# Raw patch sets in two transfers of 64 and 8 rows, borders on GpSimd, a first root of one column

## The chip, the cores and the metric

The kernel runs on one core of a Trainium2 chip. The metric is the device time of one execution in microseconds (us); the time of a kernel is the median of its runs.

## The reference

The input is a batch of 16 images of 256 channels, 28x28 pixels, in float32. Two layers replace a 3x3 convolution by soft look-up in a table: each channel's 3x3 patch is compared with 16 centroids of that channel, a softmax over the negative distances gives 16 weights, and these weigh 16 rows of a table, summed over all channels.

```python
def amm_conv3x3(x, centroids, w_sub):
    p = patches(x, 3x3, 'SAME')                        # (B, HW, C, 9)
    d = sum(p*p, -1) - 2*einsum('bncs,cks->bnck', p, centroids) + sum(centroids**2, -1)
    attn = softmax(-d, axis=-1)                        # over the 16 centroids
    lut = einsum('cks,cso->cko', centroids, w_sub)
    return einsum('bnck,cko->bno', attn, lut)          # back to (B, C, 28, 28)

h   = groupnorm(x, 32 groups, eps=1e-5)
out = relu(bn1(amm1(h)))
out = bn2(amm2(out))
out = out * sigmoid(relu(mean_hw(out) @ w1 + b1) @ w2 + b2)
result = x + relu(out + h)
```

## The kernel before

The work is cut into blocks: one image, one half of the channels (`hh`, 128 partitions) and one half of the rows (`t`, 14 rows of 28 pixels, 392 columns). `BLOCKS = ((0, 0), (0, 1), (1, 1), (1, 0))` is the order of the (hh, t) blocks of an image. In this text block 0 to block 3 are those of image 0 in layer 1, with which the program begins.

A block goes through these steps:

- Two *patch sets* (`p` 0 and 1) of 128 partitions x 3136 elements: nine taps of eight channel groups. Later blocks build them by DMA from a padded image (`patches`, L549). 
- `logits` (L578): matmuls of the patches with the centroid weights into PSUM (`lg`); `exps` (L589) on ScalarE gives `e`.
- `num_b` (L643) and `num_a` (L629): the matmuls `nb` and `na` on `e`, which form sums over centroids and numerators. `split_r`, `split_q` on ScalarE and `join_r`, `join_q` (L657, L668) on VectorE take `nb` apart; `recip` (L671), `spread` (L682, L686, shuffles) copy the reciprocal to the partitions; `scale_a` (L705, VectorE) and `scale_q` (L694, GpSimd) make the normalised weights `qp`, `qo`. `scale_a` reads `na` from PSUM and so frees its bank.
- `mix` (L720, L722, GpSimd) adds pairs of these, since the last product with the table, `product` (L713, into `acc`), is done by a scheme of seven products instead of eight on a 2x2 split; `combine` (L237, VectorE) adds table pieces for the same scheme.

**Image 0 of layer 1 is different.** Its patches are not of the normalised image: they are the raw input, laid out beforehand in `in_p0` and loaded as eight sets by `raw` (L268 to L273), and the group norm is folded into the logit weights: `tap_scale` (L397) multiplies the weights by each channel's root, `tap_shift` (L405, L408) takes the mean out of them. Nine taps of eight channels take 72 of the 128 partitions; `RAW` lists as (first row, step) which rows one transfer fills, and the constant `TAPS` which of the 16 rows of a group hold taps. A patch at the image's edge must see zero after the norm, so its raw value must be the mean: `border` (L485 to L494) adds it, once to the first and last column (L489) and once to the first or last row (L491), both on VectorE. The statistics are made by `raw_stats`, `raw_mean`, `raw_dev`, `raw_var`, `raw_means`, `raw_norm` and `raw_keep` (L427 to L483), for `k` 0 and 1, the two halves of the channels; the root is a power of -0.5 (`mhalf`) on GpSimd, of 16 columns in `raw_norm` (L473) and of one in `raw_keep` (L481). Sets 0 and 1 (block 0) and 4 to 7 (blocks 2 and 3) go into the two patch buffers, sets 2 and 3 (block 1) into the space of the table buffers `wall`.

**What sets the order.** Each engine runs its instructions in the order of the program. The start is written out by hand; then every step is entered in a list under a key (block and a fraction of it), and the program walks the sorted list. `QUEUE` holds the keys at which SyncE (SP) issues sets 2 to 7, and `BORDER` those of the eight borders. An SP issue waits while eight earlier transfers are outstanding, and for its buffer to be free. PSUM banks go by a table of tags (`EARLY`), so a block's logits wait until the last reader of their bank is done. Around these steps stand the group norm of image 1 (`gn_stats`, `gn_mean`, `gn_var` with a root at L311 and L312, `to_home1` L547) and `setup_bn` (L311, L312 on GpSimd, then L320 to L328 on VectorE: the constants of the two batch norms), entered at (6, 2.75); `keep_wd` (L411) issues two DMAs from GpSimd.

Of the kernel before, what the change touches and what calls it, by code (L numbers as in the profile page):

```python
# [12 lines left out]
ALU = mybir.AluOpType  # L13
# [4 lines left out]
P = 128  # L18
# [70 lines left out]
def kernel(  # L89
# [55 lines left out]
    def bank(name, step=None, role=None, tag=None):  # L145
        return banks(name, step, role, tag)[:, 0, :]
# [4 lines left out]
    def view(t, off, dims):  # L151
        return bass.AP(t.tensor, t.offset + off, [list(d) for d in dims])
# [274 lines left out]
    def raw_stats(k):  # L427
        gn_stats(0, k)
        rr = piece(48).rearrange("p (a n) -> p a n", a=3)
        mv = gst[0][1][:, k, :]  # L430
        for i in range(2):
# [8 lines left out]
    def raw_dev(k):  # L440
        ps, rr, mean = raws["ps", k], raws["rr", k], gst[0][1][:, k, 0:1]
        dv = piece(2)
        nc.vector.tensor_sub(dv[:, 0:1], ps[:, 0:1], mean)
        nc.vector.scalar_tensor_tensor(dv[:, 1:2], ps[:, 0:1], mean, dv[:, 0:1], op0=ALU.subtract, op1=ALU.mult)
        nc.vector.scalar_tensor_tensor(rr[:, 0], hot_sb[:, :16], dv[:, 1:2], rr[:, 2], op0=ALU.mult, op1=ALU.add)
        raws["dv", k] = dv

    def raw_var(k, ps):
        nc.tensor.matmul(ps[:, :16], lhsT=eighth, rhs=raws["rr", k][:, 0], start=True, stop=True)
        nc.tensor.matmul(ps[:, 16:17], lhsT=gmat, rhs=raws["dv", k][:, 1:2], start=True, stop=True)  # L450
        raws["pv", k] = ps

    def raw_means(k):
        ps = raws.pop(("ps", k))
        m2 = piece(16)
        nc.vector.tensor_scalar(m2, ps[:, 16:32], 2.0, None, op0=ALU.mult)
        term = piece(64).rearrange("p (a n) -> p a n", a=4)
        nc.vector.tensor_tensor(
            term, ps[:, 16:32].unsqueeze(1).to_broadcast([P, 4, 16]), hot_sb[:, 16:20].unsqueeze(2).to_broadcast([P, 4, 16]),
            ALU.mult,  # L460
        )
        gm = piece(2)
        nc.vector.tensor_copy(gm, ps[:, :2])
        raws["m2", k], raws["term", k], raws["gm", k] = m2, term, gm

    def raw_norm(k):
        ve = piece(18)
        ps = raws.pop(("pv", k))
        nc.vector.tensor_scalar(ve[:, :17], ps[:, :17], GN_EPS, None, op0=ALU.add)
# [3 lines left out]
        nc.gpsimd.tensor_tensor(sc, ve[:, :16], mhalf, ALU.pow)  # L473
        nc.gpsimd.tensor_scalar(scm, sc, hot_sb[:, 22:23], hot_sb[:, 23:24], op0=ALU.mult, op1=ALU.add)
        nc.gpsimd.tensor_tensor(ms, raws["m2", k], sc, ALU.mult)
        raws["scm", k], raws["ms", k], raws["ve", k] = scm, ms, ve

    def raw_keep(k):
        ve, gm = raws["ve", k], raws["gm", k]
        rstd, shift = (nrm[:, 0, i, k : k + 1] for i in (1, 2))  # L480
        nc.gpsimd.tensor_tensor(rstd, ve[:, 17:18], mhalf[:, :1], ALU.pow)  # L481
        nc.gpsimd.tensor_tensor(shift, gm[:, 0:1], rstd, ALU.mult)
        nc.gpsimd.tensor_scalar(shift, shift, -1.0, None, op0=ALU.mult)  # L483

    def border(u, p):  # L485
        v = flat(u["pt", p]).rearrange("p (s r w) -> p s r w", s=8, w=W)
        tm, t = raws["term", u["hh"]], u["t"]
        cols = v[:, :, :, 0 : W : W - 1]
        nc.vector.tensor_tensor(cols, cols, view(tm, 8 * p, [tm.ap[0], [1, 8], [0, RT], [16, 2]]), ALU.add)  # L489
        row = v[:, :, (RT - 1) * t, :]  # L490
        nc.vector.scalar_tensor_tensor(  # L491
            row, row, hot_sb[:, 20 + t : 21 + t], tm[:, 2 + t, 8 * p : 8 * p + 8].unsqueeze(2).to_broadcast([P, 8, W]),
            op0=ALU.mult, op1=ALU.add,
        )  # L494
# [694 lines left out]
    def at(cl, sub, f, *a, **kw):  # L1189
        jobs.setdefault((cl, sub), []).append((f, a, kw))  # L1190
# [260 lines left out]
    raw_mean(0, bank("gnp", tag=0))  # L1451
    raw_dev(0)
    sq_sum(0, 0, bank("sqp", tag=1)[:, :256])
    raw_var(0, bank("gnq", tag=3))
    sq_sum(0, 1, bank("sqp", tag=2)[:, :256])
    raw_means(0)
    sq_add(0, 0)
    raw_norm(0)
    nc.gpsimd.memset(alts[0], 1.0)
    for t in xpads:  # L1460
        nc.gpsimd.memset(t, 0.0)
    raw_keep(0)
    mean_off(0, 0, 256)
    tap_sum(0, 0, bank("tap", tag=0)[:, :256])
    sq_add(0, 1)
# [5 lines left out]
    at(-0.4, 0.6, tap_shift, 0, 1)  # L1471

    def later():
        b = banks("sqp", tag=1)
# [113 lines left out]
def _lay_out(inputs):  # L1588
# [97 lines left out]
```

## Time and profile before

| | |
|---|---|
| median of 3 runs | 2619.93 us (2618.88 to 2620.37) |
| profiled execution | 2617.88 us |
| its span | 2616.4 us |
| mean granted clock of TensorE | 0.998 |
| instructions | 85872 |

In the profile PE is TensorE's matmul, DVE is VectorE, ACT ScalarE, POOL GpSimd, and SPq SyncE's DMA queue. A row of a timeline gives the start and the busy time in us, the engine, the line, the operation, output and inputs with their shapes and the number of instructions (x), and in brackets how long the engine had been idle and what it waited for. A row of the table by stretch gives the stretch, its length, the busy time and the number of instructions of each engine, the clock that was granted to TensorE as a share of full speed, the share of the DMA engines' time in use, and GB/s. Names of `first` are pieces of one constant tile; weights, terms and scales all lie there.

### The profile page before, as it was taken

Reading aid. Unit: us, or ns where it says so; the run is one execution under the profiler, and the core shown is the slowest. Engines: PE = TensorE matmul, PEld = TensorE weight load, DVE = VectorE, ACT = ScalarE, POOL = GpSimd, SP = SyncE. Lnnn points to the kernel's source line nnn. Section 1 sums busy time; section 2 is a strip of 40 time slices with the busy share of each in tenths; the row PEclk is TensorE's granted clock in tenths of the full one; section 3 lists DMA queues with packets and bytes.
Section 4 is the critical chain, followed back from the end, with each engine's and each line's share of the span. In section 5 each row is a group of like instructions: output and inputs, shape, how many; then the busy total and the mean of one; then the engine's idle time right before and its main releaser. Section 6 shows DMA issues by size and latency. Waiting matters only on the chain.

```text
span 2616.4 us, 85872 instructions
## 1 busy us (share of the span) xinstructions
PE 2591.2 (99%) x37026; PEld 1272.7 (49%) x37026; DVE 1786.9 (68%) x3812; ACT 1368.6 (52%) x1912; POOL 1900.2 (73%) x1323
## 2 busy tenths in 40 slices
PE   7999999999999999999999999999999999999999
PEld 3444454444444444444444444444444444444445
DVE  8776656666566665666666776767777667767676
ACT  5444444444444444444454655565555555555565
POOL 5786666766568766676667777778878788787776
PEclk9999999999999999999999999999999999999999
DMA  7566656665556565655664444444444444444442
GB/s 206 136 166 177 198 149 185 170 176 173 145 144 153 168 186 174 175 145 152 170 170 107 112 115 117 130 115 113 107 130 120 121 118 106 116 128 126 116 105 66
DMA packets 213672, 372.07 MB, mean 142 GB/s; under 512 B 29880, under 2 KB 183912, under 8 KB 212712
## 3 DMA queue, kind: packets, MB, share of 16 engines
q1 hardware_dynamic: 206968, 333.75, 48.0%
q0 software_dynamic: 6176, 32.66, 3.4%
q8 instruction: 295, 4.83, 0.8%
q14 instruction: 89, 0.73, 0.1%
q10 hardware_dynamic: 144, 0.10, 0.0%
HBM read 288.46 MB, written 77.95 MB: 140 GB/s over the span
## 4 chain that ended last, share of the span: by engine, by line
PE 98%; DVE 1%; issue 0%; ACT 0%; DMA 0%; POOL 0%; ACTq 0%; DVEq 0%; POOLq 0%
PE acc L713 52%; PE lg L578 17%; PE na L629 14%; PE nb L643 14%; ACT e L589 0%; PE sep L1014 0%; DMA pt<-in_p 0%; POOL qp L722 0%; PE sep L1006 0%; DVE rb L686 0%; DMA xt<-in_x 0%; PE tap L390 0%; PE sqp L374 0%; PE sqp L343 0%; DVE qp L705 0%
## 5 line engine op out<-in xcount | busy, mean ns | idle before, releaser
L713 PE MATMUL acc<-qp,wall 128*128 128x392 f32 (+1 forms) x3088 | 1100.1, 499 | 0.6 <-issue 0.3
L589 ACT ACTIVATE e<-lg 128x784 f32<-128x784 f32 x960 | 737.5, 821 | 644.2 <-PE lg L578 641.5
L722 POOL TENSOR_TENSOR qp<-qp,qp 128x784 f32<-128x784 f32 x512 | 943.7, 1866 | 159.6 <-DVE qp L705 159.2
L713 PEld LDWEIGHTS acc<-qp,wall 128*128 128x128 f32 x3088 | 569.6, 190 | 507.4 <-issue 59.5
L686 DVE STREAM_SHUFFLE rb<-r 128x392 f32<-128x392 f32 x1024 | 550.8, 604 | 0.0
L578 PE MATMUL lg<-pt,wd 32*32 32x392 f32 x15872 | 468.9, 499 | 1.0 <-issue 1.0
L657 DVE SCALAR_TENSOR_TENSOR r<-nb,kst,r 128x392 f32<-128x392 f32 x128 | 80.1, 626 | 446.2 <-ACT r L653 445.6
L705 DVE TENSOR_TENSOR qp<-na,rb 128x784 f32<-128x784 f32 x352 | 333.8, 972 | 61.2 <-PE na L629 50.0
L629 PE MATMUL na<-e,cwa 64*32 64x392 f32 x8192 | 374.1, 492 | 0.0
L643 PE MATMUL nb<-e,cwb 64*32 64x392 f32 x8192 | 373.5, 492 | 0.4 <-ACT e L589 0.3
L694 POOL TENSOR_TENSOR qo<-qo,rb 128x392 f32<-128x392 f32 x128 | 132.5, 1035 | 296.1 <-DVE rb L682 295.7
L671 DVE RECIPROCAL r<-r 128x392 f32<-128x392 f32 x128 | 333.2, 2603 | 4.4
L694 POOL TENSOR_TENSOR qp<-qp,rb 128x784 f32<-128x784 f32 x160 | 295.9, 1860 | 3.2 <-issue 0.4
L643 PEld LDWEIGHTS nb<-e,cwb 64*32 64x32 f32 x8192 | 189.4, 107 | 175.1 <-issue 21.1
L629 PEld LDWEIGHTS na<-e,cwa 64*32 64x32 f32 x8192 | 182.6, 106 | 182.5 <-issue 74.4
L578 PEld LDWEIGHTS lg<-pt,wd 32*32 32x32 f32 x15872 | 116.1, 103 | 266.1 <-issue 230.2
L713 PE MATMUL acc<-qp,w_A 128*128 128x392 f32 x512 | 183.9, 502 | 0.0
L653 ACT ACTIVATE r<-nb,kst 128x392 f32<-128x392 f32 x128 | 86.7, 677 | 166.2 <-PE nb L643 158.6
L613 POOL TENSOR_TENSOR z<-z,mx 128x1568 f32<-128x1568 f32 x32 | 91.8, 2870 | 94.8 <-DVE mx L607 94.8
L713 PE MATMUL acc<-qo,wall 128*128 128x392 f32 (+1 forms) x386 | 158.0, 491 | 0.0
L699 ACT COPY qp<-na 128x784 f32<-128x784 f32 x160 | 130.0, 813 | 21.7 <-PE na L629 20.2
L713 PEld LDWEIGHTS acc<-qp,w_A 128*128 128x128 f32 x512 | 95.3, 191 | 83.0 <-DVE qp L705 19.8
(229 smaller groups left out, 1706.8 us busy)
## 6 DMA issues: line engine op xcount, KB each, us to landing
pt<-home SPq DMA_DIRECT2D x744, 209.0 KB
pt<-home SPq DMA_DIRECT2D x744, 104.5 KB
home<-xpad SPq DMA_DIRECT2D x30, 899.0 KB
xt<-in_x SPq DMA_DIRECT2D x30, 784.0 KB
out_dram<-y SPq DMA_DIRECT2D x31, 392.0 KB
pt<-in_p SPq DMA_DIRECT2D x24, 196.0 KB
d_wS<-st SPq DMA_DIRECT2D x12, 192.0 KB
wall<-d_wS SPq DMA_DIRECT2D x4, 576.0 KB
```

What stands on the lines that cost most here:

```text
L578: nc.tensor.matmul(bk[32 * c : 32 * c + 32, :N].rearrange("p (r w) -> p r w", w=W), lhsT=(wx[u["hh"]] if early(u) else wts["wd", u["hh"]]) ...
L589: nc.scalar.activation(eg[:, 2 * i : 2 * i + 2, :], bk[:, :, :N], AF.Exp, scale=2.0)
L613: nc.gpsimd.tensor_tensor(zk, zk, mx.unsqueeze(2).to_broadcast([P, N // 4, K]), ALU.subtract)
L629: nc.tensor.matmul(bs[32 * i : 32 * i + 32, r, :N], lhsT=wts["cwa", u["hh"]][64 * r : 64 * r + 64, mm, i, :], rhs=es[64 * r : 64 * r + 64, ...
L643: nc.tensor.matmul(bs[32 * i : 32 * i + 32, r, :N], lhsT=wts["cwb", u["hh"]][64 * r : 64 * r + 64, mm, i, :], rhs=es[64 * r : 64 * r + 64, ...
L671: nc.vector.reciprocal(u["r"], u["r"])
L686: nc.vector.stream_shuffle(rb[:, r, :], u["r"], mask_of(2 * mm + r))
L694: nc.gpsimd.tensor_tensor(q, q, u.pop(("rb", mm)), ALU.mult)
L699: nc.scalar.copy(pair(u, mm), u.pop(("na", mm))[:, :, :N])
L705: nc.vector.tensor_mul(pair(u, mm), u.pop(("na", mm))[:, :, :N], rb)
L713: nc.tensor.matmul(accs[key][:, : cols[1] - cols[0]], lhsT=wl[w][:, k, :], rhs=us["q", k][:, cols[0] : cols[1]], start=first and n == 0, s ...
L722: nc.gpsimd.tensor_tensor(pair(out_u, mm), pair(in0, mm), pair(in1, mm), ALU.subtract)
```

## The change

1. A raw set comes in two transfers of 64 and 8 rows instead of four of 16 and one of 8. The 72 rows and the bytes are the same; the taps sit in other rows of their group of 16.
2. Of the eight borders, seven go to GpSimd, as three additions each: the columns without the corner row (128 x 8 x 13 x 2), the row without its ends (128 x 8 x 26) and the two corners (128 x 8 x 2), for which the table of terms has eight planes instead of four. The border of block 0's first set stays on VectorE as it was. The keys of five borders and of the issue of set 6 change.
3. The root of the first half of the channels (`k` 0) is taken of one column per partition (`raw_root`), then spread to 16 columns by a matmul and scaled by VectorE (`raw_scales`). The second half keeps the root of 16 columns. Three memsets of GpSimd move.

```diff
-RAW = ((0, 8), (4, 8), (1, 8), (5, 8), (2, 16))
+RAW = ((0, 2), (1, 16))
...
-QUEUE = (None, None, (-0.9, 0.0), (-0.4, 0.0), (0, 1.5), (1, 1.5), (4, 1.5), (5, 1.5))
-BORDER = ((-0.5, 0.0), (-0.3, 0.0), (1, 0.97), (1, 1.9), (2, 1.6), (4, 0.5), (5, 1.1), (7, 0.2))
+QUEUE = (None, None, (-0.9, 0.0), (-0.4, 0.0), (0, 1.5), (1, 1.5), (4, 0.35), (5, 1.5))
+BORDER = ((-0.5, 0.0), (-0.3, 0.0), (1, 0.5), (1, 0.98), (2, 0.5), (3, 1.5), (4, 0.82), (6, 2.72))
...
-TAPS = ((0, 8, 5), (4, 12, 13), (1, 9, 2))
+TAPS = ((0, 8, 6), (4, 12, 14), (2, 10, 1))
...
-    eighth = piece(P)
+    eighth = hpads[1][:, :P]
...
+    def raw_root(ps):
+        ve, gm = piece(2), raws["gm", 0]
+        rr, rstd = raws["rr", 0], nrm[:, 0, 1, 0:1]
+        nc.tensor.matmul(ps[:, :1], lhsT=gmat, rhs=raws["dv", 0][:, 1:2], start=True, stop=True)
+        sq_add(0, 0)
+        nc.vector.scalar_tensor_tensor(ve[:, 0:1], ps[:, :1], GN_EPS, gm[:, 1:2], op0=ALU.add, op1=ALU.add)
+        nc.gpsimd.tensor_tensor(rstd, ve[:, 0:1], mhalf[:, :1], ALU.pow)
+
+    def raw_scales(ps):
+        rr, rstd = raws["rr", 0], nrm[:, 0, 1, 0:1]
+        nc.vector.tensor_scalar(rr[:, 0], hot_sb[:, :16], rstd, None, op0=ALU.mult)
+        nc.tensor.matmul(ps[:, 16:32], lhsT=eighth, rhs=rr[:, 0], start=True, stop=True)
+        sq_add(0, 1)
+        scm, ms = piece(16), piece(16)
+        nc.vector.tensor_scalar(scm, ps[:, 16:32], hot_sb[:, 26:27], hot_sb[:, 27:28], op0=ALU.mult, op1=ALU.add)
+        nc.vector.tensor_tensor(ms, ps[:, 16:32], raws["m2", 0], ALU.mult)
+        raws["scm", 0], raws["ms", 0] = scm, ms
...
     def border(u, p):
         v = flat(u["pt", p]).rearrange("p (s r w) -> p s r w", s=8, w=W)
         tm, t = raws["term", u["hh"]], u["t"]
-        cols = v[:, :, :, 0 : W : W - 1]
-        nc.vector.tensor_tensor(cols, cols, view(tm, 8 * p, [tm.ap[0], [1, 8], [0, RT], [16, 2]]), ALU.add)
+        first = u["hh"] == 0 and t == 0 and p == 0
+        r0, r1 = (0, RT) if first else (1 - t, RT - t)
+        eng = nc.vector if first else nc.gpsimd
+        cols = v[:, :, r0:r1, 0 : W : W - 1]
+        eng.tensor_tensor(cols, cols, view(tm, 8 * p, [tm.ap[0], [1, 8], [0, r1 - r0], [16, 2]]), ALU.add)
         row = v[:, :, (RT - 1) * t, :]
...
+        eng.tensor_tensor(
+            row[:, :, 1 : W - 1], row[:, :, 1 : W - 1],
+            tm[:, 2 + t, 8 * p : 8 * p + 8].unsqueeze(2).to_broadcast([P, 8, W - 2]), ALU.add,
+        )
+        ends = row[:, :, 0 : W : W - 1]
+        eng.tensor_tensor(ends, ends, view(tm, 16 * (4 + 2 * t) + 8 * p, [tm.ap[0], [1, 8], [16, 2]]), ALU.add)
```

On GpSimd, from the second root (of 16 columns) to the root of image 1's group norm, there stood before:

```order
27 L473 TENSOR_TENSOR first<-first,mhalf 128x16
28 L474 TENSOR_SCALAR first<-first,hot_sb 128x16
29 L475 TENSOR_TENSOR first<-first 128x16
30 L397 TENSOR_TENSOR first<-wd_174,first 128x512
31 L481 TENSOR_TENSOR nrm<-first,mhalf 128x1
32 L482 TENSOR_TENSOR nrm<-first,nrm 128x1
33 L483 TENSOR_SCALAR nrm<-nrm 128x1
34 L1507 MEMSET hpad 128x900 x2
35 L694 TENSOR_TENSOR qo_198<-qo_198,rb_559 128x392
36 L694 TENSOR_TENSOR qp_186<-qp_186,rb 128x784
37 L694 TENSOR_TENSOR qp_189<-qp_189,rb 128x784
38 L311 TENSOR_SCALAR rs_t<-gn_var 128x2
```

and on the same engine there stand now, from the last addition of the border of block 2's first set to the same root:

```order
42 L525 TENSOR_TENSOR pt_68<-pt_68,first 128x8x2
43 L725 TENSOR_TENSOR qo_192<-qo_192,rb_542 128x392
44 L725 TENSOR_TENSOR qp_180<-qp_180,rb 128x784
45 L725 TENSOR_TENSOR qp_183<-qp_183,rb 128x784
46 L512 TENSOR_TENSOR pt_69<-pt_69,first 128x8x13x2
47 L520 TENSOR_TENSOR pt_69<-pt_69,first 128x8x26
48 L525 TENSOR_TENSOR pt_69<-pt_69,first 128x8x2
49 L1537 MEMSET hpad 128x900 x2
50 L512 TENSOR_TENSOR pt_68<-pt_68,first 128x8x13x2
51 L520 TENSOR_TENSOR pt_68<-pt_68,first 128x8x26
52 L525 TENSOR_TENSOR pt_68<-pt_68,first 128x8x2
53 L311 TENSOR_SCALAR rs_t<-gn_var 128x2
```

The borders of block 2 (row 42 ends the first, rows 46 to 48 are the second) now stand around block 1's scalings (L725), and the border of block 3's first set (rows 50 to 52) ahead of the root of image 1; the memset of `hpad` moved behind the scalings. Before, nothing stood between the scalings and that root. The border of block 3's second set stands behind the mixes and the two DMA issues, ahead of the batch norm's constants:

```order
62 L753 TENSOR_TENSOR qp_180<-qp_184,qp_180 128x784
63 L411 DMA d_wd_113<-wd_159 128x512
64 L411 DMA d_wd_113<-wd_168 128x512
65 L512 TENSOR_TENSOR pt_69<-pt_69,first 128x8x13x2
66 L520 TENSOR_TENSOR pt_69<-pt_69,first 128x8x26
67 L525 TENSOR_TENSOR pt_69<-pt_69,first 128x8x2
68 L311 TENSOR_SCALAR rs_t<-vecs 128x2
69 L312 TENSOR_TENSOR bnsc_953<-rs_t,mhalf 128x2
```

so that VectorE's L326, which waits for those constants, comes behind that border too, and block 2's scalings (L736, the L705 of before) behind L326:

```order
79 L326 TENSOR_TENSOR bnsc_953<-bnsc_953,vecs 128x2
80 L327 TENSOR_TENSOR bnsh_954<-vecs,bnsc_953 128x2
81 L328 TENSOR_TENSOR bnsh_954<-vecs,bnsh_954 128x2
82 L326 TENSOR_TENSOR bnsc_961<-bnsc_961,vecs 128x2
83 L327 TENSOR_TENSOR bnsh_962<-vecs,bnsc_961 128x2
84 L328 TENSOR_TENSOR bnsh_962<-vecs,bnsh_962 128x2
85 L736 TENSOR_TENSOR qp_189<-na,rb 128x784
```

These VectorE rows follow each other as they did before; what moved is the GpSimd work that the first of them waits for.

More of the change, by code (lines that the diff above doesn't have):

```diff
@@ L430, in raw_stats @@
         mv = gst[0][1][:, k, :]
-        for i in range(2):
+        for i in range(1 + k):
             nc.vector.tensor_scalar(rr[:, 1 + i], hot_sb[:, :16], mv[:, i : i + 1], None, op0=ALU.mult)
@@ L444, in raw_dev @@
         nc.vector.scalar_tensor_tensor(dv[:, 1:2], ps[:, 0:1], mean, dv[:, 0:1], op0=ALU.subtract, op1=ALU.mult)
-        nc.vector.scalar_tensor_tensor(rr[:, 0], hot_sb[:, :16], dv[:, 1:2], rr[:, 2], op0=ALU.mult, op1=ALU.add)
-        raws["dv", k] = dv
+        if k:
+            nc.vector.scalar_tensor_tensor(rr[:, 0], hot_sb[:, :16], dv[:, 1:2], rr[:, 2], op0=ALU.mult, op1=ALU.add)
+        gm = piece(2)
+        nc.vector.tensor_copy(gm, ps[:, :2])
+        raws["dv", k], raws["gm", k] = dv, gm
     def raw_var(k, ps):
@@ L1453 @@
     sq_sum(0, 0, bank("sqp", tag=1)[:, :256])
-    raw_var(0, bank("gnq", tag=3))
+    ps = bank("gnq", tag=3)
+    raw_root(ps)
+    nc.gpsimd.memset(alts[0], 1.0)
     sq_sum(0, 1, bank("sqp", tag=2)[:, :256])
     raw_means(0)
[L1457 to L1462, printed above, removed]
     mean_off(0, 0, 256)
+    raw_scales(ps)
     tap_sum(0, 0, bank("tap", tag=0)[:, :256])
-    sq_add(0, 1)
     mean_off(0, 256, 512)
@@ L1471 @@
     at(-0.4, 0.6, tap_shift, 0, 1)
+    for t in xpads:
+        at(-0.2, 0.0, nc.gpsimd.memset, t, 0.0)
+    at(-0.2, 0.1, raw_keep, 0)
     def later():
@@ L1502 @@
     for t in hpads:
-        at(1, 1.95, nc.gpsimd.memset, t, 0.0)
+        at(3, 1.55, nc.gpsimd.memset, t, 0.0)
     for key in sorted(jobs):
@@ L1630, in _lay_out @@
         hot[p, 16:20] = dx == 0, dx == 2, dy == 0, dy == 2
-        hot[p, 20:22] = dy != 0, dy != 2
-        hot[p, 22:24] = p % 16 in rows, p % 16 not in rows
+        hot[p, 20:24] = dx == 0 or dy == 0, dx == 2 or dy == 0, dx == 0 or dy == 2, dx == 2 or dy == 2
+        hot[p, 24:26] = dy != 0, dy != 2
+        hot[p, 26:28] = p % 16 in rows, p % 16 not in rows
     for n, p in enumerate(p for first, step in RAW for p in range(first, P, step)):
```

25 lines of the change are left out of this document (13 added, 12 removed).

## The prediction

> **What bounds the kernel now.** I read the busy shares first.
>
> ```profile
> PE 2591.2 (99%) x37026; PEld 1272.7 (49%) x37026; DVE 1786.9 (68%) x3812; ACT 1368.6 (52%) x1912; POOL 1900.2 (73%) x1323
> ```
>
> TensorE works 2591.2 of 2616.4 us, so an edit pays only where PE stands idle or runs slow. The second view is the busy time of each engine by stretch, cut at the first 120 us, where all edits lie.
>
> ```profile
> core 0: us, PE busy (x) PEld busy (x) DVE busy (x) ACT busy (x) POOL busy (x), PEclk, DMA share, GB/s
> 0.00:14.40 14.40, 6.30 (x16) 3.71 (x16) 9.30 (x26) 7.90 (x5) 9.50 (x20) 1.00 0.81 203
> 14.40:22.10 7.70, 7.12 (x136) 3.41 (x136) 4.24 (x12) 5.93 (x8) 3.31 (x6) 1.00 1.06 277
> 22.10:33.30 11.20, 9.37 (x197) 3.76 (x196) 10.75 (x29) 5.84 (x8) 6.57 (x9) 1.00 0.97 231
> 33.30:42.20 8.90, 6.51 (x132) 2.52 (x133) 8.73 (x18) 3.41 (x5) 5.30 (x4) 1.00 0.98 260
> 42.20:53.40 11.20, 10.85 (x87) 5.37 (x87) 9.98 (x28) 3.89 (x6) 0.97 (x2) 0.85 0.47 146
> 53.40:64.40 11.00, 7.53 (x193) 3.01 (x192) 10.96 (x17) 6.13 (x8) 8.42 (x7) 1.00 0.55 167
> 64.40:77.50 13.10, 13.04 (x142) 5.73 (x142) 10.01 (x27) 4.83 (x7) 6.43 (x9) 0.74 0.61 161
> 82.40:120.00 37.60, 37.60 (x541) 18.59 (x542) 27.86 (x65) 16.85 (x24) 33.55 (x21) 1.00 0.59 154
> ```
>
> From 82.4 us PE is never idle (37.60 of 37.60); what the change moves there passes to the end unaltered. Before that VectorE is the full engine (10.75 of 11.20, 8.73 of 8.90, 10.96 of 11.00), and GpSimd has room in the same stretches: 6.57, 5.30, 0.97, 8.42. DMA is full until about 42 us (shares 0.97 and 0.98) and half full after. Two stretches have a lower clock. Third, PE's own timeline: the logit groups behind each gap (idle before them in brackets), and two stages behind the last.
>
> ```profile
> 14.44 5.67 PE L578 MATMUL lg<-pt,first 32*32 32x392 f32 x128 [2.37 <-issue]
> 26.38 2.76 PE L578 MATMUL lg<-wall,first 32*32 32x392 f32 x64 [0.82 <-issue]
> 33.35 0.95 PE L578 MATMUL lg<-wall,first 32*32 32x392 f32 x32 [1.00 <-ACT qp L699]
> 42.21 1.81 PE L578 MATMUL lg<-pt,first 32*32 32x392 f32 x48 [2.35 <-issue]
> 64.47 3.42 PE L578 MATMUL lg<-pt,first 32*32 32x392 f32 x64 [3.54 <-issue]
> 74.72 2.86 PE L629 MATMUL na<-e,cwa 64*32 64x392 f32 x64
> 77.52 1.00 PE L578 MATMUL lg<-pt,first 32*32 32x392 f32 x32
> ```
>
> The gaps total 10.08 us (2.37 + 0.82 + 1.00 + 2.35 + 3.54), which is what there is to win, plus the clock:
>
> ```profile
> 45.00:46.00 1.00, 1.00 (x9) 0.48 (x2) 1.00 (x1) 0.80 (x2) 0.00 (x0) 0.50 0.00 0
> 70.00:71.00 1.00, 1.00 (x3) 0.62 (x2) 1.00 (x5) 0.00 (x0) 0.35 (x1) 0.50 0.87 273
> ```
>
> Behind the gap of 2.35 PE ran part of the stretch 42.2 to 53.4 at half clock (mean 0.85: 0.15 x 11.2 = 1.7 us lost), behind that of 3.54 part of the next (mean 0.74: 0.26 x 13.1 = 3.4 us lost).
>
> **The start.** The root of 16 columns becomes one of one column.
>
> ```profile
> 8.72 2.94 POOL L473 TENSOR_TENSOR first<-first,mhalf 128x16 f32<-128x16 f32 x1 [3.75 <-DVE first L469]
> 12.16 0.42 DVE L397 TENSOR_TENSOR first<-wd,first 128x256 f32<-128x256 f32 x1 [1.37 <-POOL first L474]
> 16.69 0.60 POOL L481 TENSOR_TENSOR nrm<-first,mhalf 128x1 f32<-128x1 f32 x1
> ```
>
> One column costs 0.60 against 2.94, a gain of 2.34. Against it stands a new detour, a small DVE product, one matmul and two DVE reads of PSUM before the weights can be scaled, which I put at 1.5 us together with the DVE work queued between. So the first logits start about 0.8 earlier, at 13.7 (bounds: 0, if DVE's queue eats it, and 1.4, since VectorE's scaling waited 1.37 for GpSimd here).
>
> **The borders.** Seven of eight move from DVE (two instructions) to GpSimd (three).
>
> ```profile
> 37.44 1.54 DVE L489 TENSOR_TENSOR pt<-pt,first 128x224 f32<-128x224 f32 x1
> 39.01 1.80 DVE L491 SCALAR_TENSOR_TENSOR pt<-pt,hot_sb,first 128x224 f32<-128x224 f32 x1
> 41.24 0.42 DVE L408 TENSOR_TENSOR first<-first,tmp 128x256 f32<-128x256 f32 x1
> 49.00 0.56 DVE L489 TENSOR_TENSOR pt<-pt,first 128x224 f32<-128x224 f32 x1
> 49.59 0.45 DVE L491 SCALAR_TENSOR_TENSOR pt<-pt,hot_sb,first 128x224 f32<-128x224 f32 x1
> 61.19 2.18 DVE L489 TENSOR_TENSOR pt<-pt,first 128x224 f32<-128x224 f32 x1
> 29.81 0.22 POOL L475 TENSOR_TENSOR first<-first 128x16 f32<-128x16 f32 x1
> 35.62 1.02 POOL L694 TENSOR_TENSOR qo<-qo,rb 128x392 f32<-128x392 f32 x1 [1.90 <-DVE rb L682]
> ```
>
> On DVE a border costs 1.01 alone (0.56 + 0.45), and 3.34 at 37.44 (1.54 + 1.80). On GpSimd no border stands in the trace. A line through the rows of 16 and 392 elements gives 0.22 + 192 x 0.0021 = 0.63 for 208 elements, so 0.63 + 0.63 + 0.22, about 1.5 for cols, row and corner ends. Bounds: 1.0, DVE's time alone, and 3.3, DVE's longest; I take 1.5, since the GpSimd rows are the nearest in kind. The Trainium skill, "GPSIMD Engine Reference", section 4.1, keeps elementwise work on VectorE and calls GpSimd about twice as slow with two inputs; by that a border would cost 2.0 instead of 1.5, and the sum below would lose 1 us, two borders standing in its last chain. The row of 392 elements says less, 1.02 on GpSimd.
>
> **The sets.** Five transfers of a set become two of the same 903 KB.
>
> ```profile
> 24.45 0.49 SPq L272 DMA_DIRECT2D pt<-in_p  x1
> 28.84 0.33 SPq L212 DMA_DIRECT2D cwa<-in_cwa  x1
> 45.65 3.05 SPq L272 DMA_DIRECT2D pt<-in_p  x5
> ```
>
> SP held its issues at 24.45 and 28.84 until the sets of block 1 had landed: 4.39 us a set. No 64-row transfer of these rows is in the trace. With the engines full, the bytes set the pace, so I take the same 4.4 a set (bounds 3.3, 903 KB at the 277 GB/s of the busiest stretch, and 5.9, at the 154 GB/s of the last one). The issue time falls from 3.05 to about 1.2 a set, and two transfers rather than five count towards the outstanding ones, so SP issues earlier. That hurries nothing while DMA is full. For block 3's first set another thing counts: it goes into the buffer that block 2's first logits read, was issued at 45.65 when they ended, and they will end at about 41.8 (below). It then lands between 46.2 (41.8 + 4.4) and 50.1 (45.65 + 4.4); I take 49.6, since weights stand ahead of it in the queue.
>
> **Walking PE through it.** Block 1, first set: lands 24.4, GpSimd border to 26.0, logits 26.1 (was 26.38); the start's 0.8 shrinks to 0.3, because the set is now the limit. Second set: border done 30.4, so the gap of 1.00 closes (-1.3). Block 2, first set: before, DVE did its border (37.44 to 40.8) ahead of the last tap shifts (L408, 41.24), and both stood before logits at 42.21. Now DVE is rid of it, and GpSimd goes landed set, second root (2.9), tap scale (1.05), shift, border: 30.4 to 37.8. Logits at 38.6, -3.6, and the drop to half clock behind that gap goes too (1.7). Two stalls take its place: 1.2 us at the PSUM bank that DVE's join empties, and 1.0 at the group norm of image 1, whose DVE steps stand where they stood. So block 2's second set is at -4.2. Block 3, first set: before, the border ran on DVE at 61.19 behind products, shuffles and the combine (end 64.4); now it is done by 51.1, and PE goes straight on: 57.0 instead of 64.47, -7.5. The na group behind it comes at 64.0 instead of 74.72: -10.7, with 3.4 of clock.
>
> There the gain meets a new chain. Its order on GpSimd: border of block 3's first set, image 1's root and shift, three mixes, a scaling, two mixes, two DMA issues, border of the second set, the BN constants; then DVE's L326, behind which the scalings L736 are queued, which free the banks for block 3's second logits.
>
> ```profile
> 52.33 0.25 POOL L311 TENSOR_SCALAR rs_t<-gn_var 128x2 f32<-128x2 f32 x1 [11.77 <-DVE gn_var L526]
> 53.74 0.24 POOL L529 TENSOR_SCALAR nrm<-nrm 128x2 f32<-128x2 f32 x1
> 56.33 6.63 POOL L722 TENSOR_TENSOR qp<-qp,qp 128x784 f32<-128x784 f32 x3 [2.35 <-DVE qp L705]
> 67.01 1.24 POOL L411 DMA_DIRECT2D d_wd<-wd  x2
> 69.64 0.71 POOL L312 TENSOR_TENSOR bnsc<-rs_t,mhalf 128x2 f32<-128x2 f32 x1
> 71.16 0.16 DVE L326 TENSOR_TENSOR bnsc<-bnsc,vecs 128x2 f32<-128x2 f32 x1
> 75.72 0.97 DVE L705 TENSOR_TENSOR qp<-na,rb 128x784 f32<-128x784 f32 x1 [2.45 <-PE na L629]
> ```
>
> Border done 51.1; root and shift 1.65 (52.33 to 53.98): 52.8. Mixes to DMA issues, 11.92 (56.33 to 68.25) less 0.6, since the border that ran beside them on DVE is gone: 64.1. Border 1.5: 65.6. BN constants 2.1 (68.25 to 70.35): 67.7. The second L326 with its two followers, 0.6, and one L736, 0.97: 69.3. PE has finished na at 66.85 (64.0 + 2.86), so it waits 2.4, and block 3's second logits start at 69.3 against 77.52: **-8.2**. A gap of 2.35 was followed by half clock and gaps up to 1.00 were not, so this one likely costs 1.7 again: **-6.5**.
>
> Against the profiled execution (2617.88, span 2616.4) that is 2611.4. The median of the runs, 2619.93, lies 2.05 above it; the same gain from there gives **2613.4**.
>
> **The rivals.** *A, the sets land faster* (bound 3.3 us a set): block 1 no longer waits for its sets (1.1 us more, the start's 0.8 kept and more), the second root and block 2 follow, and PE keeps some of the -10.7 at na. GpSimd's mixes still need products that DVE makes, so it ends 2 us better, and the shorter gap may spare the 1.7 of clock: 2.0 + 1.4 beyond the forecast, about 2610. For it: fewer waits on SP. Against: the engines were full, and the bytes are the same.
>
> *B, the borders on GpSimd are dearer, or the clock falls for longer.* Each us more per border costs 2 in the last chain (two borders), and the gap of 2.4 grows with it. With 2.3 a border, 1.6 us less, and 3.4 instead of 1.7 of clock: gain 3.2, or 2616.7. For it: four-dimensional views of two elements inside have no row here. What else bears on it are the stretched DVE borders beside GpSimd's scaling, 3.34 for 1.01. The Trainium skill, "SBUF — State Buffer", section "Who interferes with whom", says that a DVE instruction with two SBUF inputs and a GpSimd one that reads SBUF share a port pair, held for a whole instruction by whichever was first; by it the GpSimd borders would be stretched in their turn by DVE's adds. The trace agrees as far as DVE goes (L489 2.18 beside mixes, 0.56 alone).
>
> *C, slower: GpSimd stands at the border of block 3's first set.* All mixes are queued behind this border, which before they were not. If 64-row transfers run at 5.9 us a set instead of 4.4, seven sets (itself the last) bring it from 49.6 to 60.1; its border ends at 61.6, and root, mixes, issues, border, constants and L736 (18.2, from 51.1 to 69.3 above) give logits at 79.8, +2.3. PE waits several us just ahead of that, and a drop like that of 3.4 follows: +5.7, about 2625.6. It decides from about 5.5 a set: seven times the 1.1 then eats the 6.5 to 8.2. Against: the transfers of before used a full queue, and one of 64 rows has enough rows for 16 engines.
>
> *D, no change at all*, the first wait being another: speaks against it that DVE, the engine unloaded, is full in each of the stretches with gaps. It would leave 2619.9.
>
> **How the numbers follow.** Forecast 0.48 at 2613.4; A 0.15 at 2610; B 0.20 at 2616.7 and D 0.05 at 2619.9; C 0.12 at 2625.6. About 0.2% (5.2 us) is what a measurement of this kernel can tell from no change: faster is below 2614.7, slower above 2625.2. Of the forecast's own spread, an unsure 1 us on each of start, borders and mixes, a sixth falls above 2614.7: faster 0.40 + 0.15 = 0.55. Same: 0.08 + 0.25 and the milder part of C (0.02) = 0.35; slower 0.10. The range 2608.5 to 2621 leaves out C and the far end of A.
>
> **What would show it.** Right: the logit groups at 14.44, 26.38, 42.21 and 64.47 move to about 13.7, 26.1, 38.6 and 57.0, with no half clock near 45; a PE gap of 2 to 3 us ahead of block 3's second logits, released by DVE's scaling, and GpSimd without a pause from its border to the BN constants. A GpSimd border sums to about 1.5. Wrong: SP's issues show over 5 us a set, or GpSimd idles behind a DMA ahead of block 3's border (C); a border of 2.5 us or more (B); no gap ahead of block 3's second logits (A).

## The result

The changed kernel takes 2613.17 us (median of 9 runs, 2611.14 to 2614.54) against 2620.28 us of the kernel before beside it (9 runs): a ratio of 0.9974, 95% interval 0.9965 to 0.9984. Run again beside other kernels it took 2612.87 us against 2617.00, a ratio of 0.998 (0.9971 to 0.9989). The profiled execution took 2614.36 us, its span 2612.9. The number came out as forecast, but by another sum: the start had the wrong sign, the sets were faster than the sum has them, a loss of clock was charged that this profile does not show, and these errors nearly cancelled.

PE's timeline of the changed kernel, the logit groups of the first blocks and the na group behind block 3's first (L609 and L660 are the L578 and L629 of before):

```profile
16.58 6.27 PE L609 MATMUL lg<-pt,first 32*32 32x392 f32 x128 [1.67 <-issue]
27.71 2.78 PE L609 MATMUL lg<-wall,first 32*32 32x392 f32 x64
40.99 1.82 PE L609 MATMUL lg<-pt,first 32*32 32x392 f32 x48
43.77 0.89 PE L609 MATMUL lg<-pt,first 32*32 32x392 f32 x16 [0.96 <-DVE qo L699]
59.20 2.77 PE L609 MATMUL lg<-pt,first 32*32 32x392 f32 x64
66.71 2.86 PE L660 MATMUL na<-e,cwa 64*32 64x392 f32 x64
71.75 0.95 PE L609 MATMUL lg<-pt,first 32*32 32x392 f32 x32 [2.19 <-issue]
```

Against the rows of before the first logits are 2.1 late, those of block 1 1.3 late, block 2's 1.2 early, block 3's first 5.3 early, the na group 8.0 early, and block 3's second logits 5.8 early (71.75 for 77.52). The gaps of 2.35 and 3.54 ahead of blocks 2 and 3 are gone; one of 2.19 stands ahead of the last row, where none was. The table by stretch shows the clock:

```profile
core 0: us, PE busy (x) PEld busy (x) DVE busy (x) ACT busy (x) POOL busy (x), PEclk, DMA share, GB/s
13.40:21.20 7.80, 5.91 (x103) 2.86 (x105) 6.35 (x16) 2.97 (x4) 4.08 (x7) 1.00 0.97 338
21.20:24.60 3.40, 3.37 (x59) 1.74 (x50) 0.11 (x1) 3.15 (x5) 1.70 (x3) 1.00 0.96 296
45.00:53.00 8.00, 7.69 (x65) 3.92 (x71) 7.42 (x26) 1.27 (x3) 2.63 (x6) 1.00 0.34 115
66.70:76.60 9.90, 7.32 (x165) 2.90 (x164) 7.50 (x19) 3.68 (x6) 8.10 (x10) 1.00 0.41 138
76.60:120.00 43.40, 43.37 (x596) 21.73 (x604) 31.30 (x78) 18.55 (x26) 37.33 (x25) 1.00 0.61 156
```

Both stretches of low clock are gone, and in this profile the gap of 2.19 was not followed by a new one (1.00 in the fourth row). From 76.6 us to 120 PE is busy throughout (43.37 of 43.40), so the 5.8 us pass on there. The other new thing is in the last column: with DMA just as full, the sets move at 338 and 296 GB/s, where it was 277 and 231.

At the start the row that matters is VectorE's L477, the spread of the root to 16 columns in `raw_scales` (one tile times one column as the scalar operand):

```profile
8.30 0.58 POOL L473 TENSOR_TENSOR nrm<-first,mhalf 128x1 f32<-128x1 f32 x1 [3.34 <-DVE first L472]
8.85 2.89 POOL L1487 MEMSET wall<- 128x3360 f32 x1
9.13 2.64 DVE L477 TENSOR_SCALAR first<-hot_sb,nrm 128x16 f32<-128x16 f32 x1
9.27 2.50 DVE L379 TENSOR_TENSOR wd<-wd,sqp 128x256 f32<-128x256 f32 x1
```

The root takes 0.58, as costed. But L477, 16 columns, takes 2.64 us and ends at 11.77, just behind GpSimd's fill of a table buffer (L1487, 8.85 to 11.74), with L379, the next instruction, behind it. The borders and the chain ahead of block 3's second logits:

```profile
21.21 0.96 POOL L512 TENSOR_TENSOR wall<-wall,first 128x208 f32<-128x208 f32 x1 [2.58 <-DMA wall<-in_p]
22.25 0.54 POOL L520 TENSOR_TENSOR wall<-wall,first 128x208 f32<-128x208 f32 x1
22.74 0.25 POOL L525 TENSOR_TENSOR wall<-wall,first 128x16 f32<-128x16 f32 x1
24.60 0.95 POOL L512 TENSOR_TENSOR wall<-wall,first 128x208 f32<-128x208 f32 x1 [1.61 <-DMA wall<-in_p]
50.38 0.94 POOL L512 TENSOR_TENSOR pt<-pt,first 128x208 f32<-128x208 f32 x1 [5.21 <-PE gnp L547]
54.67 6.65 POOL L753 TENSOR_TENSOR qp<-qp,qp 128x784 f32<-128x784 f32 x3 [0.91 <-DVE qp L736]
69.47 0.71 POOL L312 TENSOR_TENSOR bnsc<-rs_t,mhalf 128x2 f32<-128x2 f32 x1
70.22 0.16 DVE L326 TENSOR_TENSOR bnsc<-bnsc,vecs 128x2 f32<-128x2 f32 x1 [0.45 <-POOL bnsc L312]
70.69 2.73 DVE L736 TENSOR_TENSOR qp<-na,rb 128x784 f32<-128x784 f32 x3
```

A border costs 1.8 us (21.21 to 22.99), and the sets of block 1 land 3.4 us apart (24.60 less 21.21: GpSimd waits for each), not 4.4. The chain is the one that was forecast: constants, L326, the scaling L736, then PE. One wait in it was not: GpSimd stands 0.91 us for VectorE's products (L736) ahead of the mixes at 54.67.

### The profile page after: what moved, and what is told of

Same layout as the page of the kernel before. It is cut to its first block, busy times and chain, and to the rows that moved or that the text cites. A ratio compares the mean times of both kernels' runs of the same rounds, so it can differ in the third digit from the quotient of the medians.

```text
span 2612.9 us, 85829 instructions
## 1 busy us (share of the span) xinstructions
PE 2590.2 (99%) x37026; PEld 1273.7 (49%) x37026; DVE 1779.5 (68%) x3798; ACT 1369.3 (52%) x1912; POOL 1908.8 (73%) x1341
## 3 DMA queue, kind: packets, MB, share of 16 engines
q8 instruction: 295, 4.83, 0.8%
## 4 chain that ended last, share of the span: by engine, by line
PE 97%; DVE 1%; POOL 1%; issue 0%; ACT 0%; DMA 0%; SPq 0%; ACTq 0%; POOLq 0%
PE acc L744 52%; PE lg L609 17%; PE nb L674 14%; PE na L660 14%; POOL qp L753 0%; DVE rb L717 0%; DVE r L702 0%; PE sep L1045 0%; ACT e L620 0%; PE sep L1037 0%; DMA xt<-in_x 0%; DVE gn_st L424 0%; DVE qp L736 0%; DVE first L477 0%; PE tap L390 0%
## 5 line engine op out<-in xcount | busy, mean ns | idle before, releaser
L609 PE MATMUL lg<-pt,wd 32*32 32x392 f32 x15872 | 470.1, 499 | 1.0 <-DMA pt<-home 0.4
L660 PE MATMUL na<-e,cwa 64*32 64x392 f32 x8192 | 374.3, 492 | 0.0
L736 DVE TENSOR_TENSOR qp<-na,rb 128x784 f32<-128x784 f32 x352 | 333.7, 972 | 59.1 <-PE na L660 47.3
L725 POOL TENSOR_TENSOR qo<-qo,rb 128x392 f32<-128x392 f32 x128 | 131.3, 1026 | 299.3 <-DVE rb L713 298.6
L725 POOL TENSOR_TENSOR qp<-qp,rb 128x784 f32<-128x784 f32 x160 | 295.9, 1860 | 3.0
L660 PEld LDWEIGHTS na<-e,cwa 64*32 64x32 f32 x8192 | 183.0, 106 | 182.2 <-issue 73.8
L609 PEld LDWEIGHTS lg<-pt,wd 32*32 32x32 f32 x15872 | 116.7, 103 | 268.4 <-issue 241.0
```

The lines of the kernel that those rows point to most:

```text
L609: nc.tensor.matmul(bk[32 * c : 32 * c + 32, :N].rearrange("p (r w) -> p r w", w=W), lhsT=(wx[u["hh"]] if early(u) else wts["wd", u["hh"]]) ...
L660: nc.tensor.matmul(bs[32 * i : 32 * i + 32, r, :N], lhsT=wts["cwa", u["hh"]][64 * r : 64 * r + 64, mm, i, :], rhs=es[64 * r : 64 * r + 64, ...
L725: nc.gpsimd.tensor_tensor(q, q, u.pop(("rb", mm)), ALU.mult)
L736: nc.vector.tensor_mul(pair(u, mm), u.pop(("na", mm))[:, :, :N], rb)
```

## The experiments

Each is told by its trace first, since most differences between these kernels are near the width of the intervals. There is one profile of each run. Ratios are against the kernel before on the same chip.

**The fill on ScalarE.** Is it the fill that holds L477?

```diff
-    nc.gpsimd.memset(alts[0], 1.0)
+    nc.scalar.activation(alts[0].rearrange("p s n -> p (s n)"), one.to_broadcast([P, 8 * PTW]), AF.Copy)
```

> The changed kernel with the fill of the first table buffer (3360 columns of ones) moved from GpSimd to ScalarE, which is idle there. Theory: in the changed kernel VectorE's spread of the root (L477, 2.64 us for 16 columns) is held by GpSimd's fill (8.85 to 11.74), and this made the start 2.1 us late. Then L477 takes about 0.2 us here, the first logits start at about 14.2 instead of 16.58, and about 2 us of it arrive at the end: 2611. Rival: L477 waits for GpSimd's root to become visible or for something else, then it stays at about 2.6 us and the time at 2613.

2609.88 us, ratio 0.9967 (0.9955 to 0.9979). VectorE and PE:

```profile
9.13 0.23 DVE L477 TENSOR_SCALAR first<-hot_sb,nrm 128x16 f32<-128x16 f32 x1
13.41 5.67 PE L609 MATMUL lg<-pt,first 32*32 32x392 f32 x128 [0.92 <-PE tap L390]
69.73 0.95 PE L609 MATMUL lg<-pt,first 32*32 32x392 f32 x32 [2.19 <-issue]
```

L477 takes 0.23, and the first logits start 3.2 earlier, at 13.41, more than expected, since the border of block 0's first set is also rid of a neighbour (below). 2.0 of it are left at block 3's second logits; in this execution PE also ran at a clock of 0.66 from 41 to 46, which cost 1.7. The fill was the cause of L477's 2.64.

**The form of L477.** Does the fill hold any work of VectorE, or this form?

```diff
-        nc.vector.tensor_scalar(rr[:, 0], hot_sb[:, :16], rstd, None, op0=ALU.mult)
+        nc.vector.tensor_tensor(rr[:, 0], hot_sb[:, :16], rstd.to_broadcast([P, 16]), ALU.mult)
```

> The changed kernel, its fill still on GpSimd, but VectorE's spread of the root (L477) written as a product of two tiles (tensor_tensor, the root broadcast over 16 columns) instead of a tile times a scalar operand. Theory: what GpSimd's fill holds is this one form; products of two tiles ran at 0.42 us beside the same fill in the kernel before. So L477 takes about 0.2 us beside the fill, the first logits start at 13.4 to 13.7 and the time is 2610, as with the fill on ScalarE. Rival: the fill holds any VectorE work that writes this tile, then L477 stays at 2.6 us and the time at 2613.

2610.23 us, ratio 0.9971 (0.9959 to 0.9983). GpSimd, VectorE and PE:

```profile
8.77 2.89 POOL L1487 MEMSET wall<- 128x3360 f32 x1
9.05 0.17 DVE L477 TENSOR_TENSOR first<-hot_sb,nrm 128x16 f32<-128x16 f32 x1
13.26 3.30 PE L609 MATMUL lg<-pt,first 32*32 32x392 f32 x64 [0.90 <-PE tap L390]
```

The fill runs as before, and the same product, written with two tiles, takes 0.17 beside it. So it is the form of one tile with a scalar operand that was held. A scalar operand beside two tiles was not: in the kernel before the `scalar_tensor_tensor` of the border (L491) took 0.45 at 13.89, beside the same fill. Block 3's second logits start at 69.09 here, 2.7 earlier than in the changed kernel. The Trainium skill, "SBUF — State Buffer", section "Who interferes with whom", says the same of `tensor_scalar` in its two-port mode, and that a product of two SBUF tiles is not in the way of a GpSimd instruction that only writes; both rows agree. That L477 ran in this mode is inferred, since the trace does not show modes.

**The root of 16 columns**, with the fill on ScalarE, so that the root stands alone.

```diff
-        nc.gpsimd.tensor_tensor(rstd, ve[:, 0:1], mhalf[:, :1], ALU.pow)
+        raws["sc", 0], raws["ve", 0] = piece(16), ve
+        nc.gpsimd.tensor_tensor(raws["sc", 0], ve[:, 0:1].to_broadcast([P, 16]), mhalf, ALU.pow)
```

> The changed kernel with the fill on ScalarE and the first root taken of 16 columns again (the same value 16 times; the single column for later use behind it). Theory: the root's 2.3 us more arrive at the first logits in full, 15.7 instead of 13.4, since nothing else is late there, and 1 to 2 of it at the end: 2611 to 2612. Rival: the second reduction on VectorE covers part of it, and the first logits start at 14.5 or earlier, time 2610.

2611.69 us, ratio 0.9977 (0.9966 to 0.9987). GpSimd and PE:

```profile
8.38 2.94 POOL L474 TENSOR_TENSOR first<-first,mhalf 128x16 f32<-128x16 f32 x1 [3.41 <-DVE first L472]
16.40 5.66 PE L609 MATMUL lg<-pt,first 32*32 32x392 f32 x128 [1.67 <-issue]
```

The root's 2.36 arrive in full at the first logits and 0.6 more comes on top (16.40 for 13.41), since VectorE's border of block 0's first set stands beside GpSimd's border again (1.28 in this trace, 0.55 with the fill on ScalarE); nothing covers it. That is more than the 15.7 expected. The time 16.40 is also that of the changed kernel within 0.2: its short root won 2.4 us and the fill took them.

**Five transfers into the same rows.**

```diff
-RAW = ((0, 2), (1, 16))
+RAW = ((0, 8), (2, 8), (4, 8), (6, 8), (1, 16))
```

> The changed kernel with each raw set in five transfers again (four of 16 rows, one of 8), into the same rows as the two transfers. Theory: the number of transfers made the sets faster (3.4 us apart in block 1 instead of 4.4), so here they are 4.4 apart again, the second border of block 1 starts at about 28 instead of 24.6, and block 3's second logits 2 to 3 us later: 2615 to 2616. Rival: the rows, or the earlier issue, made them faster: the sets stay 3.4 apart and the time 2613.

2614.39 us, ratio 0.9984 (0.9975 to 0.9993). GpSimd's borders of block 1 and PE:

```profile
26.07 0.95 POOL L512 TENSOR_TENSOR wall<-wall,first 128x208 f32<-128x208 f32 x1 [5.80 <-DMA wall<-in_p]
30.45 0.98 POOL L512 TENSOR_TENSOR wall<-wall,first 128x208 f32<-128x208 f32 x1 [2.27 <-DMA wall<-in_p]
73.50 1.62 PE L609 MATMUL lg<-pt,first 32*32 32x392 f32 x32 [2.37 <-issue]
```

The sets are 4.38 apart again and land 4.9 and 5.9 later, more than expected for the second (30.45 for about 28), and block 3's second logits are 1.75 later. So the rows as a whole are not the reason, but the number of transfers or what each one reaches.

**Three transfers, two ways.** The same rows in two transfers of 32 and one of 8, once with the 32 spread over all partitions, once with each 32 in one half.

```diff
-RAW = ((0, 2), (1, 16))
+RAW = ((0, 128, 4), (2, 128, 4), (1, 128, 16))    # spread
+RAW = ((0, 64, 2), (64, 128, 2), (1, 128, 16))    # halves
...
-        for first, step in RAW:
+        for first, stop, step in RAW:
...
```

> The changed kernel with its 64 rows in two transfers of 32, each of every fourth partition over all 128 (0, 4, 8 ... and 2, 6, 10 ...), so three transfers a set. Theory (the ports a transfer reaches): each transfer still spreads over all the ports of SBUF, so the sets stay about 3.4 us apart in block 1. Rival (each transfer adds a fixed time): 4.4 for five and 3.4 for two make 0.33 a transfer, so 3.7 apart here and the same in the run with halves.

> The changed kernel with its 64 rows in two transfers of 32, the first into partitions 0 to 62, the second into 64 to 126 (every second one), so three transfers a set of the same bytes. Theory (the ports a transfer reaches): each transfer goes to one half of the partitions and, if the port map of the Trainium skill, SBUF — State Buffer, section Door 1, holds, to half of the ports, so the sets come slower, 4.0 to 4.4 apart. Rival (each transfer adds a fixed time): 3.7 apart, as in the run with every fourth partition.

Spread: 2611.95 us, ratio 0.9978 (0.9969 to 0.9987). Halves: 2621.42 us, ratio 1.0013 (1.0003 to 1.0022). The borders of block 1 on GpSimd, spread and then halves, and with halves also the border of block 3's first set and PE's second logits of block 3:

```profile
21.36 0.97 POOL L513 TENSOR_TENSOR wall<-wall,first 128x208 f32<-128x208 f32 x1 [2.73 <-DMA wall<-in_p]
24.63 0.95 POOL L513 TENSOR_TENSOR wall<-wall,first 128x208 f32<-128x208 f32 x1 [1.49 <-DMA wall<-in_p]
```

```profile
28.16 0.94 POOL L513 TENSOR_TENSOR wall<-wall,first 128x208 f32<-128x208 f32 x1 [6.86 <-DMA wall<-in_p]
32.99 0.95 POOL L513 TENSOR_TENSOR wall<-wall,first 128x208 f32<-128x208 f32 x1 [3.08 <-DMA wall<-in_p]
61.40 0.97 POOL L513 TENSOR_TENSOR pt<-pt,first 128x208 f32<-128x208 f32 x1 [8.03 <-DMA pt<-in_p]
82.44 1.07 PE L610 MATMUL lg<-pt,first 32*32 32x392 f32 x32 [2.99 <-issue]
```

With the same number of transfers, the same rows and bytes, the sets are 3.27 apart spread and 4.83 in halves, more than the 4.0 to 4.4 expected. The distance is not the same in every execution: in the eight profiles with two transfers a set and borders on GpSimd the two borders of block 1 start 2.7 to 3.6 apart. 4.38 and 4.83 lie outside that. A fixed time for each transfer alone, which would have made spread and halves equal, is ruled out; which partitions a transfer reaches decides. The Trainium skill, "SBUF — State Buffer", section "Door 1: The DMA port swizzle", has partitions 0 to 63 on one half of the 16 ports and 64 to 127 on the other, which agrees with the direction; no run here measures a port. By its map 16 rows at a step of 8, as in the kernel before, reach 8 ports, too, and 64 at a step of 2 all 16. Halves are the slow-set case of the prediction (its rival C) carried out: sets above 4.4 us, GpSimd standing 8.03 us at the border of block 3's first set, and the whole gain is lost.

**Only the transfers, in the kernel before.**

```diff
-RAW = ((0, 8), (4, 8), (1, 8), (5, 8), (2, 16))
+RAW = ((0, 2), (1, 16))
-TAPS = ((0, 8, 5), (4, 12, 13), (1, 9, 2))
+TAPS = ((0, 8, 6), (4, 12, 14), (2, 10, 1))
```

> The kernel before with only the transfers changed: two of 64 and 8 rows a set, taps in the new rows, borders, roots and all places as before. Theory: the faster sets alone bring little, since block 1's borders waited on VectorE's own work and block 3's border stood behind VectorE's combine: gaps of 2 to 3.5 us ahead of blocks 2 and 3 stay, and the time is within 1.5 us of 2619.5. Rival: the sets were the limit, then the time falls by 4 or more, to 2615.

2620.11 us, ratio 1.0005 (0.9996 to 1.0014). VectorE's border ahead of block 3, and PE:

```profile
61.14 1.95 DVE L237 TENSOR_TENSOR wall<-wall 128x1152 f32<-128x1152 f32 x1
63.01 2.18 DVE L489 TENSOR_TENSOR pt<-pt,first 128x224 f32<-128x224 f32 x1
66.29 4.09 PE L578 MATMUL lg<-pt,first 32*32 32x392 f32 x64 [3.54 <-issue]
```

Faster sets alone bring nothing: the border still stands behind the combine on VectorE, and the gap of 3.54 is there to the digit. This group comes 1.8 later than in the kernel before (66.29 for 64.47); 1.7 of it is clock, since PE ran at half clock for about 6.8 us behind block 2's gap here (from 44 to 51) and for 3.4 in the kernel before.

**All borders on VectorE, in the changed kernel**, at the old places.

```diff
-        first = u["hh"] == 0 and t == 0 and p == 0
+        first = True
-QUEUE = (..., (4, 0.35), (5, 1.5))
-BORDER = ((-0.5, 0.0), (-0.3, 0.0), (1, 0.5), (1, 0.98), (2, 0.5), (3, 1.5), (4, 0.82), (6, 2.72))
+QUEUE = (..., (4, 1.5), (5, 1.5))
+BORDER = ((-0.5, 0.0), (-0.3, 0.0), (1, 0.97), (1, 1.9), (2, 1.6), (4, 0.5), (5, 1.1), (7, 0.2))
```

> The changed kernel with all eight borders on VectorE, at the places of the kernel before (also the issue of set 6). Theory: GpSimd's borders closed the gaps ahead of block 2 and block 3; here gaps of 2 to 4 us come back ahead of them, and the half clock behind them: 2617 to 2619. Rival: the faster sets alone closed the gaps; then the time stays at 2613 or falls, since GpSimd's chain is shorter by two borders.

2622.91 us, ratio 1.0017 (1.0008 to 1.0026), above the expectation. GpSimd, VectorE and PE:

```profile
8.89 2.89 POOL L1487 MEMSET wall<- 128x3360 f32 x1
11.73 1.63 POOL L1537 MEMSET xpad<- 128x900 f32 x2
9.17 4.22 DVE L477 TENSOR_SCALAR first<-hot_sb,nrm 128x16 f32<-128x16 f32 x1
63.46 2.18 DVE L512 TENSOR_TENSOR pt<-pt,first 128x224 f32<-128x224 f32 x1
66.73 3.78 PE L609 MATMUL lg<-pt,first 32*32 32x392 f32 x64 [3.52 <-issue]
```

The gap ahead of block 3 is back (3.52), behind a border on VectorE that ends at 66.6, and so is half clock behind it (from 67 to 74, 3.4 us lost). So it was the borders on GpSimd, at their new places and with the earlier issue of set 6, that closed it; the run does not part these three. Ahead of block 2 the gap is 1.64, below the 2 to 4 expected. A side effect adds 0.9 at the first logits (17.43 for 16.58): without a border behind the fill on GpSimd the pads' memsets follow at once, and L477 is held until they too are through, 4.22 us.

**The constants of the batch norms in block 1**, where GpSimd and VectorE wait for a set.

```diff
-    at(6, 2.75, setup_bn)
+    at(1, 0.46, setup_bn)
```

> The changed kernel with the constants of the batch norms made in block 1, where GpSimd and VectorE are idle, not ahead of block 3's second logits. Theory: the chain border, constants, L326, scalings holds block 3's second logits for 2.2 us; without the constants VectorE's scalings start when the na matmuls end, the gap shrinks to about 0.3 and the time falls by 2 to 2611. Rival: the next wait (ScalarE's exponentials or GpSimd's mixes behind it) takes the 2 us back and the time stays at 2613.

2610.82 us, ratio 0.9969 (0.9957 to 0.9982). PE's second logits of block 3:

```profile
69.58 1.00 PE L609 MATMUL lg<-pt,first 32*32 32x392 f32 x32
```

The gap is gone and the group starts 2.2 earlier; the groups behind it keep that. So the chain of the prediction did set the place of these logits, and the constants were the link in it that could go.

**Both, on ScalarE and with the two tiles.** The constants in block 1, with the fill on ScalarE:

> The changed kernel with the fill on ScalarE and the constants of the batch norms in block 1, both. Theory: two separate limits, the start and the chain ahead of block 3's second logits, so the gains add where the first arrives (2.0 of its 3.2 us came through to block 3) and the second closes the gap of 2.2: first logits at 13.4, block 3's second logits at about 67.5 (71.75 in the changed kernel), time about 2608. Rival: they are one limit seen twice, then the time stays at 2610.

and with the fill on GpSimd and L477 as a product of two tiles, beside the changed kernel once more:

> The changed kernel with VectorE's spread of the root as a product of two tiles and the constants of the batch norms in block 1, the fill still on GpSimd. Theory: both limits fall as with the fill on ScalarE: first logits at 13.3, block 3's second logits at about 66.5 to 67 without a gap, and 4.5 to 5 us less than the changed kernel beside it. Rival: the fill on GpSimd costs something elsewhere (the border of block 0's second set behind it); then the gain beside it is 2 us.

> The changed kernel as it is, beside the next one on the same chip. Theory: its gain over the kernel before is 5.8 us by its trace (block 3's second logits), so its time stands at a ratio of 0.997 to 0.998 to the kernel before here too, and its gap of 2.2 us ahead of these logits comes back. Rival: the 7 us of the first comparison came from the chip that it ran on; then the ratio is above 0.9985.

2606.89 us, ratio 0.9961 (0.9947 to 0.9974), and 2607.28 us, ratio 0.9958 (0.9945 to 0.9972), beside 2612.87, ratio 0.998 (0.9971 to 0.9989), for the changed kernel. PE of the second:

```profile
13.38 3.28 PE L609 MATMUL lg<-pt,first 32*32 32x392 f32 x64 [0.91 <-PE tap L390]
66.96 1.00 PE L609 MATMUL lg<-pt,first 32*32 32x392 f32 x32
```

The two limits are separate, and the second version is 5.6 us below the changed kernel on the same chip, by two edited lines. The first was not run beside the changed kernel; its ratio of 0.9961 stands against 0.9974 and 0.998.

## Why the prediction was right, and where it was not

**The end of it was right.** Block 3's second logits as the place that counts, the GpSimd chain from border through mixes and constants to L326 and L736, and a PE gap of 2 to 3 us (2.19) all stand in the trace, and moving the constants showed that this chain is the limit. From the end of block 3's first border to these logits the chain was put at 18.2 us and took 19.7 (52.02 to 71.75): 0.9 is GpSimd's wait for VectorE's products, where the prediction had no pause, 0.4 the mixes and issues, 0.2 the second border. Forecast there was -8.2 and 1.7 given back to the clock, -6.5; it is -5.8, with nothing given back in this profile. The runs part it: the held start costs 2.7 at these logits (69.09 with L477 freed), the faster sets win 1.75 (73.50 with five transfers), and with the chain's 1.5 that makes 2.4 later than the 69.3 forecast, while the 1.7 of clock was not paid. That the sum came out is luck. So is the agreement of 2613.17 with 2613.4 to 0.3 us: between the medians the gain is 7.1 in the first comparison and 4.1 in the second.

**The start failed.** Forecast 0.8 earlier, it is 2.1 later; the term's detour was costed with every step but the one that stalled. The prediction does not name the fill that follows the root on GpSimd, so it stands at nothing in the sum. In the kernel before the same fill ran beside VectorE's products without harm:

```profile
12.25 2.89 POOL L1459 MEMSET wall<- 128x3360 f32 x1
12.95 0.42 DVE L408 TENSOR_TENSOR first<-first,tmp 128x256 f32<-128x256 f32 x1
```

Those had two tile inputs; L477 has one and a scalar operand. With L477 freed the first logits start at 13.26 to 13.41, 0.3 to 0.4 ahead of the 13.7 in the sum. Of the 3.2 us between 16.58 and 13.41, 2.4 are L477's and 0.7 those of the first border (below). The lower bound of the term, no gain, left out a loss without giving a reason.

**The sets failed the other way.** "The bytes set the pace" put them at 4.4 us; they take 3.4 in this profile and 2.7 in the second one of the same kernel, the fast end of the range and the condition of rival A. That the engines were full was read right, but a full engine is not one at its best rate: the rows of before moved 231 GB/s at a share of 0.97 and those of the change 296 at 0.96. At block 2 that changes nothing: with sets 4.38 apart (five transfers into the same rows) its first logits start at 40.49, and at 40.99 in the changed kernel, where 38.6 was forecast. That block 2 is 1.2 early after a start 2.1 late goes with the gaps of 0.82, 1.00 and 2.35 ahead of blocks 1 and 2, which are gone. The faster sets count at block 3: there the border of the first set starts at 50.38 instead of 53.06, and the second logits 1.75 earlier.

**The borders** were put at 1.5 and cost 1.8. The column part was too cheap, 0.95 where 0.63 was expected for 208 elements; the row, 208 elements in runs of 26, took 0.54, so the pieces of two elements are the likely cost. In block 0 a border on GpSimd (L512 at 14.46) also stands beside VectorE's own border, which then took longer: 1.27 us against 0.55 with the fill moved. GpSimd's is longer there too, 1.09, 0.71 and 0.40 for its three parts against 0.96, 0.54 and 0.25.

```profile
14.68 1.27 DVE L512 TENSOR_TENSOR pt<-pt,first 128x224 f32<-128x224 f32 x1
```

**The clock term was a rule from too few rows.** A gap of 2.35 was followed by half clock and gaps up to 1.00 were not, the prediction says. Its own rows have a gap of 2.37 ahead of the first logits, and the stretch behind that one (14.40 to 22.10) stands at 1.00. After the gap of 2.19 no half clock follows in the first profile of the changed kernel; in the second profile of the same kernel it does, and costs 1.7 us:

```profile
71.84 0.95 PE L610 MATMUL lg<-pt,first 32*32 32x392 f32 x32 [2.19 <-issue]
73.00:77.00 4.00, 4.00 (x53) 1.56 (x67) 3.86 (x9) 1.42 (x2) 4.00 (x3) 0.57 0.01 4
```

So the size of the term was right and its condition was not: the length of the gap alone does not decide. What else does stays open.

**Rivals.** The condition of A came true, but not its end: the late start hid it, and with the start freed (ratios 0.9967 and 0.9971, where A's 2610 is 0.9962) the gap of 2.2 that A would have shortened still stands. C did not happen, but the transfers in halves show that its mechanism was real. Its threshold was too high: it was to decide from about 5.5 us a set, and at 4.83 the time was already 2621.42 against 2618.34, +3.1; in its profile half clock lost 5.1 us, in two stretches ahead of block 3's second logits. B's dearer borders came to 0.3 each.

**The rest of the program.** The -5.8 at block 3 is not what every execution ends with: the first profile of the changed kernel ends 3.5 ahead of the profile of the kernel before, the second 5.8. Between about 550 and 1200 us the differences move by 1 to 3 us, in the two profiles not alike. Why was not followed up.

## What to carry to other kernels

When a step moves beside other work, ask of each engine pair which form of instruction each side uses, not only whether they overlap: one product of a tile with a scalar operand beside a fill that had done no harm before cost as much as the whole gain of a shorter root. Read a full DMA queue by its GB/s as well as its share, and shape transfers so that each one spreads over all partitions. And follow a gain to the next chain that it meets: here it ended at constants that could be made at any time before.

## What was not expected of the hardware

A GpSimd memset held VectorE's product of one tile with a scalar operand for as long as it ran, 2.64 us beside one fill and 4.22 beside three memsets, and left the same product with two tile inputs alone (0.17). Transfers of the same bytes and rows came 3.27 us apart when each spread over all partitions, and 4.83 when each went to one half. Half clock came behind a gap of 2.19 us in one execution of a kernel and not in another, and not behind one of 2.37 in the kernel before.
